# Two layers of graph attention in fp32: q and k made for two pairs of batches at once, and the order of all work planned over two pairs

## The chip, the cores and the metric

The kernel runs on one core of a Trainium2 chip. A core has TensorE for matrix products (PE in the profile, and PEld for the loading of its stationary operand), VectorE (DVE), ScalarE (ACT), GpSimd (POOL), and SyncE (SP), which here only issues transfers. The engines work side by side, each through its own queue in order, and wait for one another by semaphores. What counts is the time of one execution on the device in microseconds (us), as the median of several runs.

## What is computed

The input x holds 128 batches of 128 tokens with 512 features, in fp32; `adj` is a 128 x 128 matrix of zeros and ones, the same for all batches. Two layers follow each other, each with a residual and a layernorm:

```python
# layer 0: attention with 8 heads of 64, masked by adj
q, k, v = x @ Wq + bq, x @ Wk + bk, x @ Wv + bv
scores = einsum('bqhd,bkhd->bhqk', q, k) / sqrt(64) + (1 - adj) * -1e9
x = layernorm(x + softmax(scores) @ v @ Wo + bo)
# layer 1: edge weights from two vectors
h = x @ W
e = leaky_relu((h @ a1)[:, :, None] + (h @ a2)[:, None, :], 0.2) * adj
x = layernorm(x + elu(softmax(e) @ h + beta * h))
```

## The kernel before

**Tiling.** The kernel takes two batches at a time, a pair g of 64. The five large products q, k, v, w (the output projection with Wo) and h (the product with W) are each made for a pair by a scheme of Strassen and Winograd on 2 x 2 blocks: seven products of half-size blocks in place of eight, with sums of blocks before and after. The sums of weights are made once (`weight_sum`), those of x and of later right-hand sides for each pair by `block_sum` (L260, POOL). `product(name, g, n)` issues product n of the seven. For v, w and h (L301) it is two matmuls with a stationary block of x of 128 x 128 and 256 moving columns of the weights. For q and k (L307), which must come out with features on partitions, the weights stand still and the tokens of one batch move: four matmuls of 128 columns. The profile has two records for each matmul of the code, and its counts (`x4`, `x8`) are of records.

**Where products land.** All PSUM tiles come from one pool of 8 banks. The results are gathered in two regions of a pair: products 1, 6, 5, 3 and 2 in the main bank (product 2 in its second half), 7 and 4 in a side bank, which q and k share. After each of certain products a quarter of the result is taken out: `take_part` (ACT at L349 for v and h and at L355 for q and k, with the bias; DVE at L352 for w), and `add_block` (L365, DVE) adds what another region holds.

**x.** `load_blocks` (L81) loads a pair's x in four transfers of 128 KB, one for each block of rows, on SP's queue; `turn_x` (L240, DVE) transposes it into `xT`. `load_x` (L91) loads it once more in plain order for the residual. For pair 0, two of the four blocks go by ACT's queue. The weights come by `load_turned`; wq is issued after the blocks of pair 0.

**Attention.** `scores` (L379, PE), `mask` and `row_max` (L387, L395, DVE), `exps` and `normalise` (L401, L415, ACT, four calls of two heads each); then the probabilities are transposed by way of DRAM: `attn_write` (L422) stores a batch, `attn_read` (L427) fetches it in four transfers of 128 KB, both on SP, and `turn_attn` (L444, DVE, two halves) turns the blocks; `attend` (L454, PE) multiplies by v, `attend_evict` (L466) takes it out.

**Edges.** `edge`, `edge_exp`, `weights` make the edge weights of a pair. They too are turned by way of DRAM (`weights_write` L569, `weights_read` L576, `weights_turn` L582) before `aggregate` (L642, PE). For the last pairs, `turn_weights` (L629) uses a matmul with the identity in place of the DRAM path.

**The order.** No scheduler orders the work. Each piece is put down with a place, `at(place, fn, *args)`; all pieces are sorted by place and issued in that order, so the order on every engine's queue, SP's and POOL's included, is what the places say. `rows(g)` lists the pieces of one pair with places relative to g * STEP, `last_rows(g)` those of the last two pairs, where the projection of the last pair is made without the scheme (`plain`, `end_product` and so on, with weights loaded once more by `load_again`), and a table `other` gives other places for the first and last few pairs. `STEP` is 36.678, a pair. Single pieces, such as `weight_sum` and the loads of weights, are placed one by one. Before all of this `keep_busy` (L136) issues matmuls on the identity into a bank nobody reads.

```python
    for g in range(NG):
        lay(g)                     # at(g * STEP + place, fn, *args)
    with tc.manual_schedule():
        for _, _, fn, args in sorted(pieces, key=lambda p: p[:2]):
            fn(*args)
```

Of the kernel before, what the change touches and what calls it, by code (L numbers as in the profile page):

```python
# [13 lines left out]
P = 128  # L14
Q = 32
# [3 lines left out]
STEP = 36.678  # L19
# [3 lines left out]
def gnn_two_layers(  # L23
# [54 lines left out]
    def load_blocks(g):  # L78
        t = grp.tile([P, G, 4, P], F32, tag="xb", name=f"xblk_{g}", bufs=1)
        for a in range(4):  # L80
            (nc.scalar if g == 0 and a >= 2 else nc.sync).dma_start(  # L81
                out=t[a * Q : (a + 1) * Q].rearrange("r t b d -> r (t b) d"),
                in_=x[g * G : (g + 1) * G, :, a * P : (a + 1) * P].rearrange(
                    "t (b r) d -> r (t b) d", r=Q
                ),
            )
        return t
# [20 lines left out]
    xblk, xn = {0: load_blocks(0)}, {}  # L108
# [30 lines left out]
    early = keep_busy(15, "early")  # L139
# [11 lines left out]
    nc.gpsimd.dma_start(out=adj_sb, in_=adj)  # L151
    later = {}

    def load_later():
        later["beta"] = broadcast(cpool, beta, 1, "beta_b")
        for j in range(2):
            a_j = a1[j * D : (j + 1) * D].rearrange("f o -> (f o)")
            later["a", j] = broadcast(wk2, a_j, D, "uf")
        later["bo"] = broadcast(cpool, bo, D, "bo_b")
# [73 lines left out]
    xT, right, tx, qT, kT, vb, y, hp, main, side, oT, zT, xr = ({} for _ in range(13))  # L233
    BIAS = {"q": bq_c, "k": bk_c}
    OUT = {"q": qT, "k": kT, "v": vb, "w": y, "h": hp}

    def turn_x(g, t):
        if t == 0:
            xT[g] = grp.tile([P, NC, G * N], F32, tag="xT", name=f"xT_{g}")
        nc.vector.transpose(  # L240
            xT[g][:, :, t * N : (t + 1) * N].rearrange("p m (b r) -> p b m r", r=Q),
            xblk[g][:, t].rearrange("p b (c m) -> p b m c", c=Q),
        )

    def block_sum(name, g, n):

        if name == "x":
            b11, b12 = xT[g][:, :2, :N], xT[g][:, :2, N:]
            b21, b22 = xT[g][:, 2:, :N], xT[g][:, 2:, N:]
# [4 lines left out]
        if (name, g) not in tx:  # L254
            tx[name, g] = grp.tile(
                [P, 4, 2, N], F32, tag=f"t{name}", name=f"t{name}_{g}", bufs=2 if name == "x" else 1
            )
        t1, t2, t3, t4 = (tx[name, g][:, i] for i in range(4))
        to, a, b = {1: (t1, b12, b11), 2: (t2, b22, t1), 3: (t3, b22, b12), 4: (t4, b21, t2)}[n]
        nc.gpsimd.tensor_tensor(to, a, b, ALU.subtract)  # L260
        right[name, g] = {1: b11, 2: b21, 3: b22, 4: t4, 5: t1, 6: t2, 7: t3}

    def first_blocks(name, g):

        if (name, g) in right:
            return right[name, g]
        if name == "x":
            return {1: xT[g][:, :2, :N], 2: xT[g][:, 2:, :N]}
        src = oT if name == "w" else zT
        return {1: src[g * G][:, :2], 2: src[g * G][:, 2:]}  # L270

    def region(name, g, n):

        if n in (7, 4):
            return side[name, g]
        return main[name, g][:, 1 if n == 2 else 0]

    def product(name, g, n):
        first = False
        if n == 1:  # L280
            main[name, g] = ps_mm.tile([P, 2, HF], F32, tag="mm", name=f"p{name}_{g}")
            first = True
        if n == 7:
            if name == "k":
                side["k", g] = side["qk", g][:, 1]
            else:
                t = ps_mm.tile([P, 2, HF], F32, tag="mm", name=f"e{name}_{g}")
                side["qk", g] = t
                side[name, g] = t[:, 0]
                first = True  # L290


        out = region(name, g, n)
# [4 lines left out]
        b = first_blocks(name if name in "wh" else "x", g)[n]  # L298
        if name in "vwh":
            for c in range(2):  # L300
                nc.tensor.matmul(  # L301
                    out, b[:, c, :], a[:, c, :], start=first and c == 0, stop=(c == 1), skip_group_check=True,
                )
        else:
            for m in range(2):
                for c in range(2):
                    nc.tensor.matmul(  # L307
                        out[:, m * N : (m + 1) * N], a[:, c, m * P : (m + 1) * P], b[:, c, :],
# [4 lines left out]
    def block(name, g, i, j):  # L313

        out = OUT[name]
        if name in "qk":
            if g not in out:
                out[g] = grp.tile([P, NC, G * N], F32, tag=name, name=f"{name}T_{g}", bufs=1)
            return out[g][:, 2 * i : 2 * i + 2, j * N : (j + 1) * N]
        return whole(name, g * G + j)[:, i * HF : (i + 1) * HF]  # L320

    def whole(name, b):
        out = OUT[name]
        if b not in out:
            out[b] = wk2.tile([P, D], F32, tag=name, name=f"{name}_{b}")
# [18 lines left out]
    def take_part(name, g, n, i, j):  # L344
# [8 lines left out]
        else:  # L353
            for m in range(2):
                nc.scalar.activation(  # L355
                    dst[:, m, :], src[:, m * N : (m + 1) * N], AF.Identity,
# [3 lines left out]
    def add_block(name, g, n, i, j):  # L360

        src, dst = region(name, g, n), block(name, g, i, j)
        if name in "qk":
            src = src.rearrange("p (m n) -> p m n", m=2)
# [5 lines left out]
    def scores(b):  # L370
# [4 lines left out]
        rows = slice(i * N, (i + 1) * N)  # L375
        for m in range(HP):
            for j in range(2):
                feats = slice(j * HD, (j + 1) * HD)
                nc.tensor.matmul(  # L379
                    psc[b][j][:, m, :], qT[g][feats, m, rows], kT[g][feats, m, rows],  # L380
# [360 lines left out]
    def rows(g):  # L741

        b0, b1 = g * G, g * G + 1
        return (
            (-44.347, fetch_blocks, g), (-35.5, turn_x, g, 0), (-35.24, turn_x, g, 1),
            (-33.234, block_sum, "x", g, 1), (-29.664, block_sum, "x", g, 2),
            (-28.037, block_sum, "x", g, 3), (-27.486, block_sum, "x", g, 4),
            (-24.602, product, "q", g, 1), (-22.912, take_part, "q", g, 1, 0, 0),
            (-17.846, product, "k", g, 1), (-17.044, take_part, "k", g, 1, 0, 0),
            (-16.821, product, "q", g, 2), (-16.581, product, "q", g, 6),  # L750
            (-13.839, product, "k", g, 6), (-13.188, product, "k", g, 2),
            (-12.987, take_part, "q", g, 6, 1, 0), (-12.001, product, "q", g, 7),
            (-11.879, add_block, "q", g, 2, 0, 0), (-11.237, product, "k", g, 7),
            (-10.614, product, "q", g, 5), (-10.426, add_block, "k", g, 2, 0, 0),
            (-9.421, take_part, "k", g, 6, 1, 0), (-8.361, take_part, "q", g, 5, 1, 1),
            (-7.18, product, "k", g, 5), (-5.626, fetch_x, b0),
            (-5.405, take_part, "k", g, 5, 1, 1), (-5.039, product, "q", g, 3),
            (-4.941, add_block, "q", g, 7, 1, 1), (-4.893, add_block, "k", g, 7, 1, 1),
            (-4.838, product, "k", g, 3), (-4.757, residual, b0),
            (-3.456, take_part, "k", g, 3, 0, 1), (-3.441, take_part, "q", g, 3, 0, 1),  # L760
            (-0.228, product, "q", g, 4), (0.123, fetch_x, b1), (0.161, product, "k", g, 4),
            (0.517, add_block, "k", g, 4, 1, 0), (1.111, add_block, "q", g, 4, 1, 0),
            (2.487, scores, b0), (3.199, scores, b1), (4.193, mask, b0, 0),
            (4.492, product, "v", g, 1), (4.517, mask, b0, 1), (4.517, row_max, b0),
            (4.641, mask, b1, 0), (5.302, take_part, "v", g, 1, 0, 0), (5.86, exps, b0, 0),
            (6.834, residual, b1), (7.227, product, "v", g, 6), (7.65, product, "v", g, 2),
            (7.788, exps, b0, 1), (8.282, mask, b1, 1), (8.312, exps, b0, 2),
            (8.356, row_max, b1), (9.38, exps, b0, 3), (9.64, product, "v", g, 7),
            (9.91, add_block, "v", g, 2, 0, 0), (10.078, take_part, "v", g, 6, 1, 0),
            (10.336, row_inv, b0), (10.432, normalise, b0, 0), (10.446, normalise, b0, 1),  # L770
            (10.513, normalise, b0, 2), (11.118, product, "v", g, 5), (12.165, normalise, b0, 3),
            (12.283, exps, b1, 0), (12.823, attn_write, b0), (16.179, exps, b1, 1),
            (17.177, exps, b1, 2), (17.937, exps, b1, 3), (18.213, row_inv, b1),
            (20.003, normalise, b1, 0), (20.463, normalise, b1, 1), (21.094, normalise, b1, 2),
            (21.248, normalise, b1, 3), (21.546, attn_read, b0), (21.948, turn_attn, b0, 0),
            (22.433, attn_write, b1), (23.511, take_part, "v", g, 5, 1, 1),
            (24.964, product, "v", g, 3), (26.507, turn_attn, b0, 1),
            (27.155, add_block, "v", g, 7, 1, 1), (27.181, attn_read, b1),
            (30.486, product, "v", g, 4), (31.193, take_part, "v", g, 3, 0, 1),
            (31.929, turn_attn, b1, 0), (32.334, turn_attn, b1, 1),  # L780
            (32.982, add_block, "v", g, 4, 1, 0), (36.883, attend, b1), (38.699, attend, b0),
            (39.543, attend_evict, b0), (39.643, attend_evict, b1),
            (40.299, block_sum, "w", g, 1), (40.441, block_sum, "w", g, 2),
            (41.662, block_sum, "w", g, 3), (42.036, product, "w", g, 1),
            (42.978, product, "w", g, 2), (44, take_part, "w", g, 1, 0, 0),
            (44.174, add_block, "w", g, 2, 0, 0), (45.529, block_sum, "w", g, 4),
            (46.326, product, "w", g, 6), (46.362, product, "w", g, 7),
# [387 lines left out]
```

## Time and profile before

| what | value |
|---|---|
| median of 3 runs (lowest to highest) | 2377.61 us (2377.54 to 2379.04) |
| profiled execution, its own time | 2378.15 us |
| span of its profile | 2376.4 us |
| granted TensorE clock, mean | 0.998 |
| start of pair 0's first q product | 10.28 us |
| start of pair 0's scores | 28.84 us |
| end of the last matmul | 2369.28 us |
| issue of the last store | 2373.85 us |

The span is the time from the first to the last recorded event; the execution's own time has 1.75 us more around it. The steps are alike from the third pair to the third from the end. An engine's busy time is the sum of its records. Since matmuls are pipelined and their ends are modelled, the records of TensorE overlap: what a matmul costs is read from the distance between two starts. A line of the timeline names start, duration, engine, source line, operation, what it writes and reads, the tile and a count; where the engine stood idle before it, the idle time and what ended it stand in brackets. The page's larger groups:

```profile
L355 ACT ACTIVATE kT<-pk,bias_c 128x128 f32<-128x128 f32 x512 | 160.2, 364 | 202.2 <-PE pk L307 143.2
L349 ACT COPY v<-pv 128x256 f32<-128x256 f32 x256 | 94.6, 369 | 84.4 <-PE pv L301 59.9
L352 DVE TENSOR_TENSOR w<-pw,x 128x256 f32<-128x256 f32 x252 | 106.3, 422 | 97.3 <-PE pw L301 90.8
L387 DVE SCALAR_TENSOR_TENSOR s<-psc,amask 128x512 f32<-128x512 f32 x256 | 168.6, 680 | 0.7 <-PE psc L379 0.7
L307 PEld LDWEIGHTS pk<-xT,wk_sb 128*128 128x128 f32 x1024 | 129.1, 192 | 4.2 <-DMA wk_sb<-in_L_gnn_Wk_dram 0.6
```

After the bar stand the busy time of the group in us, the mean of one instruction in ns, and the idle time of the engine ahead of them with what ended most of it.

### The profile page before, as it was taken

The numbers are of one execution on the slowest core, as the hardware profiler recorded it, in microseconds if no ns is written. First come the engines' busy times: TensorE is split into PE (matmuls) and PEld (weight loads), VectorE is DVE, ScalarE is ACT, GpSimd is POOL, SyncE is SP. The second block draws the span as 40 slices with busy tenths as digits, with TensorE's granted clock in tenths as the row PEclk, the third lists the DMA queues.
The fourth block names the chain that finished last, engine by engine and source line by source line (L and its number), as shares of the span: only waits on it lengthen the run. The fifth ranks groups of instructions, "written<-read, shape, count | busy, mean of one in ns | idle before, by whom it ended". The sixth has DMA issues, their size and how long they took to land.

```text
span 2376.4 us, 50868 instructions
## 1 busy us (share of the span) xinstructions
PE 2354.4 (99%) x17703; PEld 2177.5 (92%) x17703; DVE 1961.7 (83%) x4390; ACT 1591.1 (67%) x5763; POOL 865.5 (36%) x1044
## 2 busy tenths in 40 slices
PE   8999999999999999999999999999999999999998
PEld 8998999999999999999999999999999999999996
DVE  7788788888888888888888888888888888888887
ACT  4675666766766667667666676676666766766665
POOL 6243333433433333334334333343343333433422
PEclk9999999999999999999999999999999999999999
DMA  6333334334343343343443433424434334344432
GB/s 192 108 100 112 116 101 125 107 105 134 92 120 119 107 118 108 108 128 92 121 122 103 119 108 111 126 92 121 123 103 119 107 112 125 92 120 122 116 115 74
DMA packets 256121, 269.83 MB, mean 114 GB/s; under 512 B 57372, under 2 KB 204840, under 8 KB 255480
## 3 DMA queue, kind: packets, MB, share of 16 engines
q1 hardware_dynamic: 254992, 265.45, 37.8%
q8 instruction: 140, 2.29, 0.4%
q14 instruction: 117, 0.96, 0.1%
q0 software_dynamic: 304, 0.85, 0.1%
q10 hardware_dynamic: 568, 0.27, 0.0%
HBM read 157.62 MB, written 108.85 MB: 112 GB/s over the span
## 4 chain that ended last, share of the span: by engine, by line
PE 96%; DMA 1%; DVE 1%; ACT 1%; issue 0%; SPq 0%; POOLq 0%; POOL 0%; DVEq 0%; ACTq 0%
PE pq L307 12%; PE pk L307 12%; PE pv L301 12%; PE ph L301 11%; PE pw L301 11%; PE eq L307 9%; PE psc L379 5%; PE po L454 5%; PE pz L642 5%; PE eh L301 5%; PE ew L301 4%; PE ev L301 4%; DMA xblk<-in_x_dram 1%; DMA wq_sb<-in_L_gnn_Wq_dram 0%; ACT s L401 0%
## 5 line engine op out<-in xcount | busy, mean ns | idle before, releaser
L435 POOL TENSOR_TENSOR x<-x,bo_b_in 128x512 f32<-128x512 f32 x128 | 163.6, 1279 | 863.3 <-DMA x<-in_x_dram 863.3
L401 ACT ACTIVATE s<-s,nmax 128x128 f32<-128x128 f32 x1024 | 396.9, 396 | 61.4 <-DVE nmax L395 61.3
L415 ACT ACTIVATE sb<-s,rinv 128x128 f32<-128x128 f32 x1024 | 325.3, 392 | 0.0
L355 ACT ACTIVATE kT<-pk,bias_c 128x128 f32<-128x128 f32 x512 | 160.2, 364 | 202.2 <-PE pk L307 143.2
L355 ACT ACTIVATE qT<-pq,bias_c 128x128 f32<-128x128 f32 x512 | 160.6, 368 | 157.6 <-PE pq L307 157.6
L505 DVE SCALAR_TENSOR_TENSOR ya<-w,wa_row 128x512 f32<-128x512 f32 x256 | 223.9, 875 | 4.4
L401 ACT ACTIVATION_READ_ACCUMULATOR s<-s,nmax 128x1 f32 x1024 | 199.2, 195 | 0.0
L466 ACT ACTIVATE oT<-po,bias_c 128x128 f32<-128x128 f32 x512 | 139.5, 382 | 80.5 <-PE po L454 80.5
L352 DVE TENSOR_TENSOR w<-pw,x 128x256 f32<-128x256 f32 x252 | 106.3, 422 | 97.3 <-PE pw L301 90.8
L444 DVE STREAM_TRANSPOSE attnT<-ab 128x512 f32<-128x512 f32 x256 | 172.7, 694 | 6.8 <-DMA ab<-scr 6.6
L387 DVE SCALAR_TENSOR_TENSOR s<-psc,amask 128x512 f32<-128x512 f32 x256 | 168.6, 680 | 0.7 <-PE psc L379 0.7
L395 DVE TENSOR_REDUCE nmax<-s 128x8 f32<-128x1024 f32 x128 | 156.1, 1220 | 4.3
L349 ACT COPY h<-ph 128x256 f32<-128x256 f32 x252 | 93.8, 372 | 94.1 <-PE ph L301 94.0
L349 ACT COPY v<-pv 128x256 f32<-128x256 f32 x256 | 94.6, 369 | 84.4 <-PE pv L301 59.9
L240 DVE STREAM_TRANSPOSE xT<-xblk 128x512 f32<-128x512 f32 x128 | 139.4, 1108 | 7.9 <-DMA xblk<-in_x_dram 7.9
L657 DVE SCALAR_TENSOR_TENSOR u<-h,x 128x512 f32<-128x512 f32 x126 | 87.1, 692 | 63.8 <-ACT h L349 61.6
L260 POOL TENSOR_TENSOR tx<-xT 128x256 f32<-128x256 f32 x128 | 94.7, 741 | 119.8 <-PE psc L379 97.1
L301 PE MATMUL pv<-wv_sb,xT 128*128 128x256 f32 x512 | 137.5, 392 | 0.0
L307 PE MATMUL pq<-xT,wq_sb 128*128 128x128 f32 x1024 | 135.9, 276 | 1.2 <-DMA wq_sb<-in_L_gnn_Wq_dram 1.2
L307 PE MATMUL pk<-xT,wk_sb 128*128 128x128 f32 x1024 | 134.8, 275 | 0.6 <-DMA wk_sb<-in_L_gnn_Wk_dram 0.4
L307 PEld LDWEIGHTS pq<-xT,wq_sb 128*128 128x128 f32 x1024 | 130.1, 193 | 4.5 <-issue 1.3
L307 PEld LDWEIGHTS pk<-xT,wk_sb 128*128 128x128 f32 x1024 | 129.1, 192 | 4.2 <-DMA wk_sb<-in_L_gnn_Wk_dram 0.6
(677 smaller groups left out, 6352.6 us busy)
## 6 DMA issues: line engine op xcount, KB each, us to landing
scr<-sb SPq DMA_DIRECT2D x128, 512.0 KB
ab<-scr SPq DMA_DIRECT2D x512, 128.0 KB
x<-in_x_dram SPq DMA_DIRECT2D x128, 256.0 KB
xblk<-in_x_dram SPq DMA_DIRECT2D x254, 128.0 KB
out_dram<-u SPq DMA_DIRECT2D x126, 256.0 KB
pb<-s2d SPq DMA_DIRECT2D x62, 128.0 KB
attd<-att SPq DMA_DIRECT2D x62, 128.0 KB
ab<-attd SPq DMA_DIRECT2D x248, 32.0 KB
```

Of the source, the lines that this page charges most:

```text
L301: nc.tensor.matmul(out, b[:, c, :], a[:, c, :], start=first and c == 0, stop=(c == 1), skip_group_check=True,)
L307: nc.tensor.matmul(out[:, m * N : (m + 1) * N], a[:, c, m * P : (m + 1) * P], b[:, c, :], start=first and m == 0 and c == 0, stop=(c == 1) ...
L349: nc.scalar.copy(dst, src)
L355: nc.scalar.activation(dst[:, m, :], src[:, m * N : (m + 1) * N], AF.Identity, bias=BIAS[name][:, 2 * i + m : 2 * i + m + 1],)
L387: nc.vector.scalar_tensor_tensor(s_t[b][:, j * HP : (j + 1) * HP, :], psc[b][j], SCALE, amask.rearrange("p (o n) -> p o n", o=1).broadcast ...
L395: nc.vector.tensor_reduce(nmax[b], s_t[b], AX.X, ALU.max, negate=True)
L401: nc.scalar.activation(s_t[b][:, h, :], s_t[b][:, h, :], AF.Exp, bias=nmax[b][:, h : h + 1], accum_out=rsum[b][:, h : h + 1],)
L415: nc.scalar.mul(sb[b][:, :, h, :], s_t[b][:, h, :].rearrange("p (b c) -> p b c", c=Q), rinv[b][:, h : h + 1],)
L435: nc.gpsimd.tensor_tensor(xr[b], xr[b], later["bo"], ALU.add)
L444: nc.vector.transpose(attnT[b].rearrange("p h (a r) -> p a h r", r=Q)[:, rows], ab[b].rearrange("p a (h c) -> p a h c", c=Q)[:, rows],)
L466: nc.scalar.activation(oT[b][:, c, :], src[:, c, :], AF.Identity, bias=bv_c[:, c : c + 1])
L505: nc.vector.scalar_tensor_tensor(z, y[b], 1.0, wa_row[j], ALU.mult, ALU.mult, accum_out=s12[g][:, i, j : j + 1])
```

## The change

q and k are made once for two pairs. `xT` and the sums of x become two single tiles with a slot for each pair of two (g % 2), and a product of q or k moves both slots' columns of a block, 256, past each stationary block: four matmuls (eight records) of 256 columns for two pairs, where there were twice four (twice eight records) of 128. Its two halves of output fill a bank; so product 2 gets a bank of its own (`two`), and q and k each have their own side bank. `take_part` for q and k takes 256 columns an instruction, `add_block` 512. `qT` and `kT` hold two pairs, and v has four buffers in place of two. v, w and h are made for each pair as before.

The plan now covers two pairs: `STEP` is 72.624 for two, `rows(g)` has one list for even and one for odd g (only the even one has the products of q and k), `last_rows` and the table `other` are new, and so are the places of the single pieces. At the start, the blocks of pair 1 are loaded (all four on SP) between those of pair 0 and wq, into a buffer of `attnT`; `load_later` (adj, beta, bo and a, by POOL's queue) moves behind the first eight sums of blocks; `keep_busy` issues 20 in place of 15.

```diff
-STEP = 36.678
+STEP = 72.624
     def load_blocks(g):
-        t = grp.tile([P, G, 4, P], F32, tag="xb", name=f"xblk_{g}", bufs=1)
+        if g == 1:
+            t = wk2.tile([P, H, N], F32, tag="attnT", name="xblk_1")
...
-    xblk, xn = {0: load_blocks(0)}, {}
+    xblk, xn = {0: load_blocks(0), 1: load_blocks(1)}, {}
...
-    early = keep_busy(15, "early")
+    early = keep_busy(20, "early")
...
+    xT_all = cpool.tile([P, NC, G, 2, N], F32, tag="xT", name="xT")
+    xs_all = cpool.tile([P, 4, 2, 2, N], F32, tag="tx", name="tx")
...
+    def factor(name, g, n):
+        if name in "qkv":
+            b11, b12, b21, b22, (t1, t2, t3, t4) = x_blocks(g % 2 if name == "v" else None)
+            return {1: b11, 2: b21, 3: b22, 4: t4, 5: t1, 6: t2, 7: t3}[n]
...
     def region(name, g, n):
         if n in (7, 4):
             return side[name, g]
+        if name in "qk":
+            return (two if n == 2 else main)[name, g]
         return main[name, g][:, 1 if n == 2 else 0]
...
     def product(name, g, n):
+        first = n in (1, 7) or (n == 2 and name in "qk")
+        if first:
+            t = ps_mm.tile([P, 2, HF], F32, tag="mm", name=f"p{n}{name}_{g}")
...
                     nc.tensor.matmul(
-                        out[:, m * N : (m + 1) * N], a[:, c, m * P : (m + 1) * P], b[:, c, :],
+                        out[:, m, :], a[:, c, m * P : (m + 1) * P], b[:, c, :],
...
                 nc.scalar.activation(
-                    dst[:, m, :], src[:, m * N : (m + 1) * N], AF.Identity,
+                    dst[:, m, :], src[:, m, :], AF.Identity,
...
     def rows(g):
+        if g % 2 == 0:
+            return (
...
+                (-30.238, product, "k", g, 1), (-28.77, block_sum, "x", g, 1),
...
+                (1.517, scores, b0), (1.537, scores, b1), (1.631, product, "v", g, 1),
...
+                (30.784, attn_write, b1), (33.944, attn_read, b1),
...
+                (37.62, attend, b0), (37.64, attend, b1),
```

In the list for odd g, with places from the same start of the two pairs, the fetch of row blocks stands at -40.984 and the fetches of x for the pairs around it stand close by; by its place the fetch of the next odd pair's blocks falls between `attn_write` and `attn_read` of the even pair's second batch. In the new `last_rows`, three products of w stand between the edge weights of pair 61 and their `aggregate`, and `end_max`, `end_sum` and `end_stats` of both last batches stand in one row behind the last `end_exp`.

## The prediction

> **What bounds the kernel now.** I read the page's busy shares first, then the chain of waits, then the TensorE timeline of a step in mid-run, then the queues that feed it, and last the two ends.
>
> ```profile
> PE 2354.4 (99%) x17703; PEld 2177.5 (92%) x17703; DVE 1961.7 (83%) x4390; ACT 1591.1 (67%) x5763; POOL 865.5 (36%) x1044
> ...
> PE 96%; DMA 1%; DVE 1%; ACT 1%; issue 0%; SPq 0%; POOLq 0%; POOL 0%; DVEq 0%; ACTq 0%
> PE pq L307 12%; PE pk L307 12%; PE pv L301 12%; PE ph L301 11%; PE pw L301 11%; PE eq L307 9%; PE psc L379 5%; PE po L454 5%; PE pz L642 5%; PE eh L301 5%; PE ew L301 4%; PE ev L301 4%; DMA xblk<-in_x_dram 1%; DMA wq_sb<-in_L_gnn_Wq_dram 0%; ACT s L401 0%
> ```
>
> TensorE is busy 99% and 96% of the chain is TensorE itself, so the kernel is bound by the time its matmuls take; q and k (pq, pk, eq) are a third of it. No other engine is above 83%. In the chain the scores of successive pairs start at 961.07, 997.57 and 1034.07: a step of 36.50 us, without a wait of TensorE.
>
> The timeline of TensorE shows what one product costs (start, duration, line, output, count of matmuls):
>
> ```profile
> 1000.46 1.89 PE L301 MATMUL pw<-wo_sb,oT 128*128 128x256 f32 x8
> 1002.18 1.03 PE L301 MATMUL pv<-s_v,tx 128*128 128x256 f32 x4
> 1003.04 1.03 PE L301 MATMUL pv<-wv_sb,xT 128*128 128x256 f32 x4
> ...
> 1028.44 1.05 PE L307 MATMUL pq<-xT,s_q 128*128 128x128 f32 x8
> 1029.33 1.06 PE L307 MATMUL pk<-xT,s_k 128*128 128x128 f32 x8
> 1030.22 1.06 PE L307 MATMUL eq<-tx,wq_sb 128*128 128x128 f32 x8
> 1031.12 1.06 PE L307 MATMUL eq<-tx,wk_sb 128*128 128x128 f32 x8
> ```
>
> Durations overlap, so the price is the distance from start to start. The profile counts two records for a matmul of the code; I count records as matmuls. Four of 256 columns: 0.865 (1002.18 to 1003.04 and on), eight of them 1.729. Eight of 128 columns: 0.8925 (1028.44 to 1031.12 in three).
>
> **What the skill says.** The Trainium skill, "TensorE: Matmul & The Clock Gate", section "Wait — 56ns, not 53.3ns?", names a fixed cost of about 2.5 ns for each matmul besides its columns. The trace agrees in kind and shows more: 111.6 ns for 128 columns and 216.1 for 256 make 2 x 111.6 - 216.1 = 7 ns a matmul. I use 7. The same page, section "What's actually happening", says that an idle window of 3.4 us halves TensorE's clock until a busy one has passed; the page here shows a dip of the granted clock after the idle start, and the first q products at 10.28 take nearly double for 3.4 us. "DMA: Bandwidth & Descriptors", section "Issuing engines are not separate DMA queues", says that all transfers share 16 engines and interleave; the trace has all softmax traffic, loads and stores on SP's queue.
>
> **The change, part by part.**
>
> *Products of q and k.* Each of the 14 products of two pairs was 2 x 0.8925 and becomes eight matmuls of 256 columns, 1.729: 0.056 less. 14 x 32 double steps x 0.056 = **-25.1 us**. Nothing in v, w, h, scores, attend or aggregate changes on TensorE. The double step is 73.00 and becomes 72.2. The operand side is not a hindrance by what is seen: the same shape, 128x128 by 256 columns, runs for v, w and h at this price; weight loads (192 ns in the group rows) fit beneath 216 ns. Bounds: 0 saved, if the weight load hid the difference anyway, to 25.1.
>
> *Evictions.* ACT's q and k parts become 8 instructions for two pairs in place of 16, each of 256 columns (0.37 as v's copy) against 0.315: about 2 us less ACT in 73. DVE's additions, 6 of 128x512 (0.68 from PSUM, as the mask) against 12 of 128x256 (0.42): 1 us less. Both engines lie beneath TensorE: worth nothing by themselves.
>
> *Banks.* Product 2 of q and k has its own bank and each has its own side bank: up to six of eight for q and k alone. I followed in TensorE's order each product that opens a bank and what must have read the bank before: the first product of w waits for an addition of h, k's first for the next addition of h, q's and k's second for the masks of the scores. By the durations above each reader ends 0.4 to 1 us ahead. I take 0; the far end goes to the range.
>
> *Softmax of the even pair.* Here the order is tighter. In the step before, the second batch's probabilities go out at 1056.17, 22.1 after its scores' start; they return as:
>
> ```profile
> 1056.17 0.34 SPq L422 DMA_DIRECT2D scr<-sb  x1
> 1056.56 1.27 SPq L726 DMA_DIRECT2D out_dram<-u  x2
> ...
> 1059.22 1.81 SPq L427 DMA_DIRECT2D ab<-scr  x4
> ...
> 1065.28 1.29 DVE L444 STREAM_TRANSPOSE attnT<-ab 128x512 f32<-128x512 f32 x2
> ```
>
> The write is T. Its data lands at T+2.67, the reads are issued from T+3.05, the last lands at T+7.64; turning takes 1.29 and attend starts at 1068.61, T+12.4. After the change q and k of the next two pairs, 24.2 us, all stand behind the odd pair's scores. Behind the even pair's scores lie v of two pairs and the w, h and aggregates that fall there, and only 33.3 us of TensorE work from them to the even pair's attend (34.5 before). ACT reaches the second batch's last normalise about 24.5 after the scores: 3.6 until mask and row maximum are there, 16.4 of its own work (8 pairs of exps of 0.775, 8 normalise of 0.61, ten others) and some 4.5 of waits for v, h and the second row maximum. That leaves 8.8 to attend's first batch, 9.75 to the second, which is the one in question. Needed: the reads plus 1.3. On SP, between this write and its reads, now stand the loads of four row blocks and one x (768 KB, where two stores of 512 KB stood). They delay no issue, since the write takes 2.67 anyhow, but their data goes ahead of the reads: 256 KB more at about 300 GB/s is 0.85, so the last read lands at T+8.5 and the chain ends at T+9.8 against 9.75. Bounds: 0.8 to spare if they interleave as before, 1.05 late if all 1.28 MB moves at the 228 GB/s of the start's slice from T+2.67 with 1.2 to complete. I take 0, the middle, knowing there is no cover.
>
> *The head.*
>
> ```profile
> 10.28 2.05 PE L307 MATMUL pq<-xT,wq_sb 128*128 128x128 f32 x8 [1.24 <-DMA wq_sb<-in_L_gnn_Wq_dram]
> ...
> 15.12 1.05 PE L307 MATMUL pk<-xT,wk_sb 128*128 128x128 f32 x7 [0.36 <-DMA wk_sb<-in_L_gnn_Wk_dram]
> ```
>
> wq is issued at 1.66 and lands at 10.15. Now four block loads (0.48 each to issue, 512 KB) go ahead of it on SP, so it lands at 11 to 13.5; wk, issued after the first transposes, at about 17. Broadcasts on POOL's queue move behind the first sums, which takes bytes from the same window. But from then TensorE has 24.2 us of q and k and three products of v with operands in place, 26.8, while before it waited again (0.36, 0.35, 0.28, 0.48, 0.55). Scores of pair 0 stood at 28.84 behind 14.2 us of such work, 14.6 lost; now a start at 12.3, 26.8 of work and 1.7 of half clock make 40.8, 14.0 lost: -0.6. With a late wk +2. I take **+0.7**.
>
> *The tail.* Before, TensorE waits 5.1 us from the last v to its end:
>
> ```profile
> 2334.48 0.43 PE L536 MATMUL pb<-ident,s_in 128*128 128x128 f32 x2 [1.20 <-DVE s_in L513]
> ...
> 2359.54 1.13 PE L671 MATMUL plh<-wk_sb,zT 128*128 128x256 f32 x4 [0.90 <-ACT zT L649]
> ```
>
> In it the edge weights of pair 61 are written at 2314.46 and aggregated at 2322.70, 8.24 later, covered by products of v and w. In the new order only three products of w (2.6 us) and some waits of theirs stand between: about 4 to 5 uncovered. With the other waits of the new order 10.7 in place of 5.1: **+5.6**. After the last matmul (end 2369.28) the last store is issued 4.4 later, because DVE has done most of batch 126 by then. The new order puts maxima, sums and statistics of both batches in one row: 4 x 0.38 + 4 x 0.41 + 4 x 0.43, two aggregates, norms and the inverse root between, about 8 and 1.5 until the first may start: 9.5, **+4.9**. An idle window over 3.4 us may halve the clock once, 1.7 us, with chance a half: **+0.8**.
>
> *Sum.* Span 2376.4 - 25.1 + 0.7 + 5.6 + 4.9 + 0.8 = 2363.3. The profiled execution took 2378.15, 1.75 more than its span and 0.54 more than the median 2377.61; so +1.2: 2364.5, rounded **2365**.
>
> **Rivals.**
> - *A: the gain is given back at the ends and in small waits.* Stalls of 0.4 in each double step on bank readers, or a head 8 us later because wq and wk wait behind the blocks: 2364.5 + 12.4 = 2377. For it: slack at h's addition is 0.4. Against: with ACT and DVE relieved by 3 us, readers come earlier.
> - *B, slower: the even pair's reads come late.* 1.0 us in each of 31 double steps is +31: 2395. It decides against the change from (25.1 - 12)/31 = 0.42 us late. For it: the budget of 9.75 against 9.8, and reads of new blocks just ahead. Against: before, the reads left in 4.6 us behind 512 KB of stores.
> - *C: a cheap tail and head.* DVE takes batch 126 first in effect and the edge round trip takes 6 in the empty machine: 10 less, 2355.
> - *D: wide q and k products are no cheaper*: 2389. Against it are v's own rows.
>
> **Numbers.** Forecast 0.55 (2358 to 2373), A 0.12, B 0.22, C 0.07, D 0.04. 0.2%, 4.75 us, is what a measurement of this kernel tells from no change: faster is below 2372.9, slower above 2382.4. Faster: 0.54 + 0.07 = 0.61. Slower: 0.20 of B, 0.04 of D and 0.01 of A: 0.25. Same: 0.14. The range 2356 to 2388 leaves out half of C, two thirds of B and half of D, 0.20.
>
> **What would show it.** Right: product starts of q and k 1.73 apart; scores of every second pair 72.2 apart; no TensorE idle before attend of even pairs; an idle of about 4 before an aggregate near the end; over 9 us from the last matmul to the last store. Wrong: idle in front of attend, its releaser the transposes or the reads (B); idle in front of a product with an addition or mask as releaser (A); products at 1.78 (D); scores of pair 0 later than 43 (head).

## The result and the profile after

| | before | changed |
|---|---|---|
| median, 21 runs each | 2377.61 us (2376.19 to 2379.73) | 2382.73 us (2379.08 to 2384.99) |
| ratio, 95% interval | | 1.0019 (1.0013 to 1.0025) |
| profiled execution | 2378.15, span 2376.4 | 2379.08, span 2377.3 |
| double step (two pairs) in mid-run | 73.00 | 72.56 to 73.89 |
| start of pair 0's scores | 28.84 | 40.50 |
| end of the last matmul to the end of the span | 7.1 | 9.8 |

The change made the kernel 5.1 us slower, where 12.6 less had been forecast. The profiled execution of the changed kernel is the fastest of its 21, so what is read from it is some 3.6 us short of the usual run, and the clock seems to be part of that: the 7 executions at its mean granted clock of 0.998 average 2381.0 us, the 14 at 0.996 or 0.997 2383.2. In the kernel before, the steps are 36.50 a pair from pair 8 on (single earlier ones go to 39.3), not yet from the third.

The page of the changed kernel, its busy shares and its chain of waits:

```profile
PE 2334.0 (98%) x14129; PEld 2046.6 (86%) x14129; DVE 1857.1 (78%) x4198; ACT 1501.5 (63%) x5251; POOL 857.4 (36%) x1044
...
PE 80%; DVE 9%; DMA 7%; SPq 2%; issue 1%; ACT 1%; DVEq 0%; POOLq 0%; POOL 0%; ACTq 0%
```

TensorE's busy time fell by 20.4 us, but its share of the chain fell from 96% to 80%: the chain now leaves TensorE, passes through transfers, SP's queue and VectorE, and comes back. A busy share of 98% hides that. TensorE's waits in the changed kernel, summed (engine, line, what it waited for: us, times, longest):

```profile
PE po L472 <- DVE attnT L462: 17.8, 30, 1.5
PE pz L660 <- DVE mv_c L498: 3.6, 1, 3.6
PE p1q L325 <- DVE wk_sb L216: 3.3, 1, 3.3
PE psc L397 <- DVE kT L383: 2.3, 1, 2.3
```

Attend waits 30 times, once in nearly every double step, for the turned probabilities. One such place in TensorE's timeline:

```profile
919.95 1.03 PE L318 MATMUL p1h<-s_h,zT 128*128 128x256 f32 x4
920.82 1.03 PE L318 MATMUL p7h<-w_sb,th 128*128 128x256 f32 x4
921.77 1.09 PE L472 MATMUL po<-attnT,v 128*64 128x128 f32 x16
923.17 1.09 PE L472 MATMUL po<-attnT,v 128*64 128x128 f32 x16 [0.30 <-DVE attnT L462]
924.19 2.06 PE L397 MATMUL psc<-kT,qT 64*128 64x128 f32 x32
...
927.14 1.89 PE L325 MATMUL p1k<-xT,wk_sb 128*128 128x256 f32 x8
928.87 1.89 PE L325 MATMUL p1q<-xT,wq_sb 128*128 128x256 f32 x8
930.60 1.89 PE L325 MATMUL p2k<-xT,wk_sb 128*128 128x256 f32 x8
```

It is attend of the even pair, second batch, the prediction's tight place; all 30 waits are at such places. The two attends take 2.42 from 921.77 to 924.19 where an undisturbed pair takes 1.90: 0.30 of idle and 0.22 more that the idle column does not show, since a wait also breaks the overlap of matmuls (undisturbed, a batch starts 0.95 after the one ahead of it, whose record is 1.09 long). Below it the wide products start 1.73 apart, as forecast.

SP's queue, then pieces of the chain, at the same place:

```profile
912.68 0.34 SPq L440 DMA_DIRECT2D scr<-sb  x1
913.11 2.33 SPq L86 DMA_DIRECT2D xblk<-in_x_dram  x4
915.54 0.40 SPq L96 DMA_DIRECT2D x<-in_x_dram  x1
916.03 1.80 SPq L445 DMA_DIRECT2D ab<-scr  x4
```

```profile
917.40 4.29 DMA ab<-scr
...
922.44 0.68 DVE attnT L462
923.12 0.04 issue
923.17 1.09 PE po L472 x16
```

The write T is at 912.68. The block and x loads follow, the reads leave at T+3.35, the last takes 4.29 and lands at T+9.0; VectorE turns it and attend starts at T+10.5, while TensorE had reached attend's first batch at T+9.1. On VectorE the wait for reads of probabilities is 67.2 us in the whole run, where it was 6.6 before; about 47 us of it stand before the even pairs' second batches.

### The profile page after: what moved, and what is told of

Read it like the earlier page. It is cut to its first block, busy times and chain, and to the rows that moved or that the text cites. A ratio compares the mean times of both kernels' runs of the same rounds, so it can differ in the third digit from the quotient of the medians.

```text
span 2377.3 us, 42885 instructions
## 1 busy us (share of the span) xinstructions
PE 2334.0 (98%) x14129; PEld 2046.6 (86%) x14129; DVE 1857.1 (78%) x4198; ACT 1501.5 (63%) x5251; POOL 857.4 (36%) x1044
## 4 chain that ended last, share of the span: by engine, by line
PE 80%; DVE 9%; DMA 7%; SPq 2%; issue 1%; ACT 1%; DVEq 0%; POOLq 0%; POOL 0%; ACTq 0%
PE p1w L318 10%; PE p1q L325 9%; PE p1k L325 9%; PE p1v L318 7%; PE p1h L318 6%; DMA ab<-scr 5%; PE psc L397 5%; PE pz L660 5%; PE p7k L325 5%; PE p7q L325 5%; PE p7w L318 4%; PE po L472 4%; PE p7v L318 3%; PE p7h L318 2%; PE p2k L325 2%; PE p2q L325 2%
## 5 line engine op out<-in xcount | busy, mean ns | idle before, releaser
L369 ACT COPY h<-p1h 128x256 f32<-128x256 f32 x252 | 93.3, 370 | 244.1 <-PE p1h L318 209.6
L462 DVE STREAM_TRANSPOSE attnT<-ab 128x512 f32<-128x512 f32 x256 | 169.4, 691 | 68.0 <-DMA ab<-scr 67.2
L369 ACT COPY v<-p1v 128x256 f32<-128x256 f32 x256 | 94.0, 367 | 167.6 <-PE p1v L318 167.6
L372 DVE TENSOR_TENSOR w<-p1w,x 128x256 f32<-128x256 f32 x252 | 104.4, 414 | 114.7 <-PE p1w L318 114.6
L375 ACT ACTIVATE kT<-p1k,bias_c 128x256 f32<-128x256 f32 x256 | 106.3, 467 | 74.8 <-PE p1k L325 74.8
L472 PE MATMUL po<-attnT,v 128*64 128x128 f32 x2048 | 133.1, 277 | 17.8 <-DVE attnT L462 17.8
L472 PEld LDWEIGHTS po<-attnT,v 128*64 128x64 f32 x2048 | 109.8, 137 | 47.2 <-DVE attnT L462 28.0
L375 ACT ACTIVATE qT<-p1q,bias_c 128x256 f32<-128x256 f32 x256 | 106.3, 466 | 54.5 <-PE p1q L325 52.6
L397 PE MATMUL psc<-kT,qT 64*128 64x128 f32 x2048 | 132.1, 279 | 2.3 <-DVE kT L383 2.3
L318 PE MATMUL p1v<-wv_sb,xT 128*128 128x256 f32 x512 | 134.2, 385 | 0.1
L318 PE MATMUL p1w<-wo_sb,oT 128*128 128x256 f32 x504 | 131.9, 385 | 0.0
```

The costliest lines, as they stand in the source:

```text
L318: nc.tensor.matmul(out, b[:, c, :], a[:, c, :], start=first and c == 0, stop=(c == 1), skip_group_check=True,)
L369: nc.scalar.copy(dst, src)
L375: nc.scalar.activation(dst[:, m, :], src[:, m, :], AF.Identity, bias=BIAS[name][:, 2 * i + m : 2 * i + m + 1],)
L397: nc.tensor.matmul(psc[b][j][:, m, :], qs[feats, m, :], ks[feats, m, :], start=True, stop=True,)
L462: nc.vector.transpose(attnT[b].rearrange("p h (a r) -> p a h r", r=Q)[:, rows], ab[b].rearrange("p a (h c) -> p a h c", c=Q)[:, rows],)
L472: nc.tensor.matmul(po[b][j * HD : (j + 1) * HD, m, :], vb[b][:, h * HD : (h + 1) * HD], attnT[b][:, j * HP + m, :], start=True, stop=True,)
```

## The experiments

Each run is timed against the kernel before on the same chip (its median there was 2377.96 both times); the changed kernel's row is from its own comparison, where the kernel before had 2377.61. An interval of the ratio that leaves out 1 is a difference clear of noise. The landing of the last read is measured from the issue of the write, for the even pair's second batch; it is the mean of 25 double steps, batches 17 to 113, from the trace's records of the transfers' ends, in us.

| run | median, us | ratio (95% interval) | write landed | reads issued | last read landed |
|---|---|---|---|---|---|
| before, the same place in pairs | 2377.96 | 1 | 2.75 | 3.08 | 7.91 (7.29 to 9.06) |
| changed | 2382.73 | 1.0019 (1.0013 to 1.0025) | 3.09 | 3.35 | 9.27 (8.88 to 10.21) |
| blocks before the write, x after the reads | 2380.49 | 1.0012 (1.0005 to 1.0019) | 4.41 | 4.43 | 9.07 |
| x after the reads | 2367.32 | 0.9955 (0.9942 to 0.9967) | 3.11 | 3.15 | 8.58 |
| blocks and x after the reads | 2358.65 | 0.9920 (0.9906 to 0.9934) | 2.66 | 2.68 | 7.43 |

My theory 1 after the result was that attend is late because its reads come late, and these because of the loads on the same transfer engines. Theory 2 was that ScalarE's work up to the write is late by itself, theory 3 that the loads can't be elsewhere without being late for their own use.

**Blocks before the write.** Order only; nothing is left out.

```diff
-            (-40.984, fetch_blocks, g), (-36.959, turn_x, g, 0)
+            (-43.0, fetch_blocks, g), (-36.959, turn_x, g, 0)
...
-            (31.726, fetch_x, b0)
+            (34.1, fetch_x, b0)
```

> The changed kernel with two transfers moved in every double step: the four row-block loads go ahead of the even pair's second probability write, the one x load behind its reads. Theory 1 (the reads of that batch queue behind 768 KB of loads, and attend waits for them): the last read lands at 7 to 7.7 us after the write in place of 9.0, attend's wait (0.5 us on average in the profile, and about 0.2 of restart) is gone in all double steps, the even-to-odd step is 35.5, and the time falls by 20 to 27, to 2356 to 2363. Theory 2 (ScalarE's chain up to the write is what is late, or attend's order on VectorE): no more than 3 less, about 2380. Theory 3 (the blocks are now early but the x transposes behind them collide with the attention's turning): 2370 to 2380, with new waits of the first k product.

Measured 2380.49: no more than theory 2 allows, so by its number theory 1 had failed. The trace says why:

```profile
1057.38 1.85 SPq L86 DMA_DIRECT2D xblk<-in_x_dram  x4
1059.66 0.34 SPq L440 DMA_DIRECT2D scr<-sb  x1
1064.82 1.73 SPq L445 DMA_DIRECT2D ab<-scr  x4
```

The loads are issued ahead of the write, but only 2.3 us ahead, so their bytes are still moving: the last of them lands 4.2 after the write's issue. This write lands 5.1 after its issue (4.4 on average), the reads wait for it, and the last one lands at 9.07 on average, hardly before 9.27. Attend still waits 25 times, 16.8 us in all. I had moved the issue and not the transfer.

**Products of 128 columns in the new plan.** Each q and k product is cut in two.

```diff
-                    nc.tensor.matmul(
-                        out[:, m, :], a[:, c, m * P : (m + 1) * P], b[:, c, :],
-                        start=first and m == 0 and c == 0, stop=(c == 1),
+                    for s in range(2):
+                        cols = slice(s * N, (s + 1) * N)
+                        nc.tensor.matmul(
+                            out[:, m, cols], a[:, c, m * P : (m + 1) * P], b[:, c, cols],
+                            start=first and m == 0 and c == 0 and s == 0, stop=(c == 1),
...
```

> The changed kernel with its plan as it is, but each q and k product issued as eight matmuls of 128 columns in place of four of 256, into the same banks. Theory 1 (the wide products save 0.056 a product, and the loss is made elsewhere): 448 x 0.056 = 25 us more, 2405 to 2409, product starts 1.785 apart, and the same waits of attend in the other half of the double step. Rival (wide products are no cheaper): 2383, starts as in the changed kernel.

Measured 2409.92 (ratio 1.0136, 1.0122 to 1.0150), 27.2 above the changed kernel where 25 was expected. Starts of products that follow each other:

```profile
1015.00 1.95 PE L327 MATMUL p1k<-xT,wk_sb 128*128 128x128 f32 x16
1016.78 1.95 PE L327 MATMUL p1q<-xT,wq_sb 128*128 128x128 f32 x16
1018.57 1.95 PE L327 MATMUL p2k<-xT,wk_sb 128*128 128x128 f32 x16
```

1.785 apart against 1.73. The wide products do save what the prediction said. Attend's waits are there too, and somewhat longer (20.3 us, 31 times, against 17.8), so not all of the 27.2 is the products; the odd half of the double step, where no attend waits, is 37.78 in place of 36.95, 0.83 for the 14 products. So the gain exists and something else eats it.

**The kernel before, with the blocks ahead of the reads.**

```diff
-            (-44.347, fetch_blocks, g), (-35.5, turn_x, g, 0), (-35.24, turn_x, g, 1),
+            (-49.4, fetch_blocks, g), (-35.5, turn_x, g, 0), (-35.24, turn_x, g, 1),
```

> The kernel before with one move: the four row-block loads of every pair go between the second batch's probability write and its reads. Theory 1 (late reads cost only where attend follows the write by less than they take): reads land some 1 to 2 us later after the write (7.64 becomes 8.6 to 9.6), attend came 12.4 after the write and still does, time 2376 to 2380. Rival (loads ahead of the reads cost in themselves, wherever they stand): 0.5 us or more in each of 62 pairs, over 2405.

Measured 2422.31 (1.0190, 1.0176 to 1.0204), 44 us more, the rival's number. I had expected nothing, because attend came 12.4 after the write. The write landed at 2.77, but the reads were issued only at 5.34 and the last landed at 10.11 on average: 2.3 and 2.2 later than in the kernel before, so what made them late here is the time that SP's queue spends on what stands ahead of them. TensorE does not wait for attend there at all. VectorE's timeline does the explaining:

```profile
1045.76 1.30 DVE L444 STREAM_TRANSPOSE attnT<-ab 128x512 f32<-128x512 f32 x2 [1.14 <-DMA ab<-scr]
1046.99 0.38 DVE L365 TENSOR_TENSOR v<-ev,v 128x256 f32<-128x256 f32 x1
1047.30 0.59 DVE L594 SCALAR_TENSOR_TENSOR ev<-pb,s_in,adj_sb 128x128 f32<-128x128 f32 x2
...
1059.12 0.41 DVE L365 TENSOR_TENSOR v<-pv,v 128x256 f32<-128x256 f32 x1
```

The turning transpose waits 1.14 for its reads, and VectorE then has 13 us of work without a gap; the addition of v at its end is late, the copy of v on ScalarE behind it, and TensorE waits for that copy 33 times. Start by start, the two profiles differ by 43.7 us: about 27 of it stand before that product of v and about 11 before the scores, which wait for an addition of q on VectorE. The room was not the 12.4 to the consumer, but the 9.1 to the transpose's turn in VectorE's queue (1065.28 in the prediction's lines). My expectation left out what is queued behind the waiting instruction. So late reads cost in this kernel as well, by way of VectorE's queue; loads that make no read late were not tried in it.

**Blocks and x behind the reads.**

```diff
-            (-40.984, fetch_blocks, g), (-36.959, turn_x, g, 0)
+            (-38.64, fetch_blocks, g), (-36.959, turn_x, g, 0)
...
-            (31.726, fetch_x, b0)
+            (34.1, fetch_x, b0)
```

> The changed kernel with the four row-block loads and the one x load of every double step issued behind the reads of the even pair's second batch, not between its write and them. Theory 1 (what stands on the transfer engines between write and reads makes the reads late; putting blocks ahead of the write only made the write land at 4.4 in place of 3.1): last read at 7.6 to 8.0 after the write in place of 9.27, attend's wait gone in most double steps, 2358 to 2366; the blocks land later, so the x transposes on VectorE wait some 0.4, which costs at most 0.4 a step. Theory 3 (the blocks are now the late ones, and the first k product behind the x transposes waits): 2370 to 2385, with waits of the first product of k in place of attend's.

Measured 2358.65: 24.1 below the changed kernel and 19.3 below the one before, in theory 1's interval. The last read lands at 7.43, a little earlier than the 7.6 to 8.0 expected. Its timelines of SP, of VectorE and of TensorE:

```profile
1049.82 0.34 SPq L440 DMA_DIRECT2D scr<-sb  x1
1052.46 1.75 SPq L445 DMA_DIRECT2D ab<-scr  x4
1054.31 1.86 SPq L86 DMA_DIRECT2D xblk<-in_x_dram  x4
```

```profile
1056.31 2.48 DVE L462 STREAM_TRANSPOSE attnT<-ab 128x512 f32<-128x512 f32 x4
1058.71 0.39 DVE L383 TENSOR_TENSOR v<-p7v,v 128x256 f32<-128x256 f32 x1
1059.70 1.13 DVE L248 STREAM_TRANSPOSE xT<-xblk 128x512 f32<-128x512 f32 x1 [0.60 <-DMA xblk<-in_x_dram]
...
1062.39 1.08 DVE L248 STREAM_TRANSPOSE xT<-xblk 128x512 f32<-128x512 f32 x1
```

```profile
1058.91 1.97 PE L472 MATMUL po<-attnT,v 128*64 128x128 f32 x32
1060.81 2.06 PE L397 MATMUL psc<-kT,qT 64*128 64x128 f32 x32
...
1063.76 1.89 PE L325 MATMUL p1k<-xT,wk_sb 128*128 128x256 f32 x8
```

Attend's two batches are one row again, without idle. The wait has moved to the x transposes as theory 3 said, 0.60, but the second of them ends at 1063.47, 0.29 before TensorE comes to the first k product, and TensorE does not wait. Nearly all double steps are 72.17 (35.22 and 36.95), and TensorE is 94% of the chain. This settles theory 2 as well: the write leaves 23.2 after its batch's scores here as in the changed kernel, so ScalarE is as late as it was and the stalls are gone all the same. Start by start, the two profiles (the same 14129 records in the same order) differ by 21.8 us, and 20.4 of it stand at attend.

**Only x behind the reads.**

```diff
-            (31.726, fetch_x, b0)
+            (34.1, fetch_x, b0)
```

> The changed kernel with only the x load (256 KB) moved behind the reads, the four block loads left between write and reads. Theory 1, by bytes: last read at 8.3 to 8.7 in place of 9.27, half of the stalls gone, 2364 to 2373. Theory 3 does not apply, since the blocks come as before. If the write's own landing and the issue of the blocks on the queue set the reads and not the bytes: reads at 9.0 to 9.3 and 2380 or more.

Measured 2367.32, inside theory 1's interval: 256 KB less ahead of the reads make them land at 8.58, and most double steps lose nothing. The step from 9.27 to 8.58 is worth 15.4 us, that from there to 7.43 only 8.7: once the reads are in time for most double steps, earlier is worth little. Attend still waits 12 times here, 7.1 us, against 4 times and 2.8 with the blocks moved too; and some of the 8.7 may be the clock, which this run's profile shows at half for 6.8 us near the end and the other's does not.

**The end.** u of the last two batches in another buffer, and batch 126 finished on VectorE ahead of 127.

```diff
-            u[b] = wk2.tile([P, D], F32, tag="uf", name=f"u_{b}")
+            t = wk2.tile([P, H, N], F32, tag="attnT", name=f"u_{b}")
+            u[b] = t.rearrange("p h n -> p (h n)")[:, :D]
...
-            (95.19, end_max, b1, 1), (95.55, end_sum, b1, 1), (95.97, end_max, b1, 0),
+            (91.0, end_max, b0, 1), (91.1, end_sum, b0, 1), (91.2, end_stats, b0, 1),
...
```

> The changed kernel with only the end altered: the last two batches' u go to a buffer of the transposed probabilities, so that they do not wait for the stores of the pair before, and VectorE finishes batch 126 ahead of 127. Theory 1 (VectorE idles 3.5 us for a store and then does both batches in a row): the last store is issued 4.4 to 7 after the last matmul in place of 9, the time falls by 2 to 4. Rival (the last exponential sets the end anyway): within 1 us of the changed kernel.

In the changed kernel, VectorE waited for a store of the pair before to release the buffer:

```profile
2367.37 0.42 DVE L700 SCALAR_TENSOR_TENSOR u<-plh,x 128x256 f32<-128x256 f32 x1 [3.50 <-DMA out_dram<-u]
```

With the edit that wait is gone and the span ends 7.1 after the last matmul in place of 9.8, 2.7 less. The median was 2378.30 (0.9999, 0.9990 to 1.0007), 4.4 below the changed kernel; the trace accounts for 2.7 of it. The edit changes buffer and order at once, so the share of each is open.

The same edit together with the loads behind the reads:

> The loads behind the reads, and the end of e4 (other buffer for the last u, batch 126 ahead of 127). The two gains lie in different parts of the run and should add up: the time of the first of these three less 3 to 5; by theory 1 2354 to 2362, below both kernels.

Measured 2358.52 (0.9916, 0.9903 to 0.9930). Below both kernels, but not 3 to 5 below the run without the new end. Its trace has the end at 7.1 after the last matmul too, but the last matmul itself came 4.6 later in this execution. Some 3 of that are single waits in the first five pairs and the last ones; 1.6 are the clock. The same aggregate near the end, first in the run without the new end, then in this one:

```profile
2306.22 2.02 PE L660 MATMUL pz<-attT,x 128*128 128x128 f32 x16 [3.51 <-DVE mv_c L498]
2309.26 2.89 PE L660 MATMUL pz<-attT,x 128*128 128x128 f32 x16 [3.53 <-DVE mv_c L498]
```

After the second wait the granted clock is 0.5 for 3.4 us, from 2310.2 on; after the first it stays at 1. Whether the 2.7 comes through in the median is open: four and five runs that scatter by 1 to 5 us don't tell.

## Why the prediction was wrong

- *Products of q and k, -25.1.* Right. Without stalls the double step is 72.17 against the 72.2 forecast: 0.83 x 31 = 25.7. The narrow run's odd half gives the same 0.83.
- *Evictions and banks, 0.* Right: no product waits for a bank in mid-run.
- *Softmax of the even pair, "I take 0, the middle, knowing there is no cover".* This is the step that failed. Place, direction and order of events were right, and the size was wrong by the 0.75 us that decides. The budget to the second batch was taken as 9.75; attend starts at 10.0 after the write where nothing waits (blocks and x behind the reads). The chain was taken as 8.5 + 1.3 = 9.8 and is 10.76 on average in the changed kernel: the last read at 9.27, turning 1.3, and 0.2 between them and attend's start.
- The reads land 0.77 later than I took, and the runs say which terms were off. The base: I read 7.64 off one step, while the mean over the kernel before is 7.91 and single steps go to 9.06 (+0.27). The blocks: I set 512 KB of loads equal to the 512 KB of stores that stood there, but with only the blocks ahead the last read lands at 8.58 against 7.91 (+0.67, across two plans, so other traffic may have a part). x's 256 KB: 0.69 by the run that moves it, against the 0.85 taken (-0.16). I had also written that the loads delay no issue. The reads leave at 2.68 with no loads ahead, at 3.15 with the blocks, since the write itself then lands later, and at 3.35 with x too; from there the last one takes 4.75, 5.43 and 5.92.
- Taking 0 was the second fault, since the cost is one-sided: a step in which reads come early gives nothing back, so a mean near the limit is not a cost of 0. Nor does the idle column show all of it: with 0.17 to 0.18 of idle the even half is 35.61 to 35.62 against 35.22, 0.40.
- The sum of it is (2382.73 - 2358.65)/31 = 0.78 us a double step. The slower rival B had the mechanism, and its turning point of 0.42; it stood at 0.22, though the sum left no cover at all.
- *Head, +0.7.* Near. Pair 0's scores start at 40.50, where the sum had 40.8 without a late wk and 2 more with one. q starts at 11.46. TensorE then waits 2.3 for k once (`psc` on `kT` above), which the sum lacked; its idle up to pair 8's scores is 8.3 in place of 9.4. The dip of the clock named in the prediction is too short for the page's slices, which all show 9; the trace has 0.50 from 10.1 to 13.6.
- *Tail, +5.6 and +4.9.* The edge weights' round trip leaves TensorE 3.6 idle (4 to 5 forecast). From the scores of the last even pair on its idle is 9.3 in place of 4.5, so 4.8 more where 5.6 was forecast (the 5.1 taken for the kernel before is 4.5 in the trace from the last v on). The end takes 2.7 more where 4.9 was forecast; its cause was half right, since the store's buffer, which I did not see, holds VectorE for 3.5.
- Without the stall the forecast of 2365 would have been 6 too high: the tail costs 7.5 where 11.3 were taken, and head and products did a little better than forecast. Of the 11.3, 0.8 were for a half clock. It does not come in the changed kernel's profile or in that of blocks and x behind the reads, but it comes in the five other profiles with the new plan, behind the same wait of 3.5, for 3.4 or 6.8 us. The prediction gave it a half.

## What to carry to other kernels

When a bound engine's work becomes shorter, list every round trip that it used to cover and compare its budget with the spread of its duration over the whole run, not with one instance: at zero slack the late steps cost and the early ones give nothing back. A load placed between a write and the read of the same data was paid for three times here, on the issuing queue, in the write's landing and in the read's data. Moving it behind the reads won that back; issuing it 2.3 us ahead of the write did not, since its bytes were still moving when the write came, and farther ahead was not tried. And the slack of a late arrival ends at the first in-order queue that waits for it, not at the engine that uses it in the end.

## What the runs showed of the hardware

Loads in flight slow a write: the 512 KB write landed in 2.66 with nothing issued close behind it, in 3.09 with loads issued behind it, in 4.41 with loads issued just ahead. A wait of TensorE of 0.17 lengthened the step by 0.40, so the idle column understates it by about 0.2 for such a wait. After a wait of TensorE of 3.5 us the granted clock fell to 0.5 in five of seven profiles with that wait, and did not in the other two. Executions of one program differ: 21 runs of the changed kernel spread over 5.9 us and those of the kernel before over 3.5.
